# A two-layer 5-tap scan network on one core: the identity made first, weights loaded further on, the first group's lower rows stored further on, and the second quarter of a right scan loaded from ScalarE's queue

## The chip, the cores and the metric

One NeuronCore of a Trainium2 chip. The metric is the device time in microseconds (us) of the whole kernel, lower is better. Everything is 32-bit floating point.

## The reference

The input `x` is 32 images of 48 channels, 64 rows and 128 columns. Two layers of the same form follow each other; the core of one is

```python
def step(w, b):
    def f(carry, inp):
        nxt = inp + conv1d(carry, w, b)     # 5 taps along the line, 48 x 48 channels
        return (nxt, nxt)
    return f
D = scan(step(down_w, down_b), rows 1..63 of gn(x))          # from row 0 down
U = scan(step(down_w, down_b), back over D, rows 62..0)      # and up again
R = scan(step(right_w, right_b), columns 1..127 of U)        # from column 0 right
L = scan(step(left_w, left_b), back over R)                  # and left again
x = x + L
```

where `gn` is a group normalization over 16 groups of channels for each image. A scan is serial: a row (or column) needs the one before it, convolved along its length. In one layer there are 126 row steps and 254 column steps.

## The kernel before

**Groups and phases.** The images are cut into four groups of 8. A row scan handles one group (`rows`, layer, group): the three output tiles of a step are 128 x 128 matmuls, nine products for a step (`PRODUCTS`), and three VectorE instructions (L660) add bias and input and write the row back into SBUF, from where the next step reads it. A column scan handles a pair of groups (`cols`, layer, pair). `PHASES` lists the order: rows of groups 0 and 1, columns of pair 0, rows of group 2 in layer 0, rows of group 0 in layer 1 and so on, twelve phases in all. A row phase has 126 steps, a column phase 254; the text counts steps through the whole program (phase 1 begins after step 126, phase 2 after 252, phase 3 after 506, phase 6 after 884, phase 7 after 1138). In the profile a step's PSUM tile is named after layer, group or pair and direction: `step_00d`, `step_00u` are layer 0, group 0, down and up; `step_00r`, `step_00l` are layer 0, pair 0, right and left.

**Order of the work.** Around the scan everything else (loads, stores, statistics, normalization) is put on an agenda: `at(t, fn, ...)` says before which step a piece of work is written into the program. `in_order` keeps the program's order on each engine, so a piece never overtakes an earlier one on the same engine or DMA queue; the time t of a piece is only its place in that order. An engine or queue that has work behind its t runs late, and one that is ahead of its t may run a piece as soon as its inputs are there. Nearly all DMAs are issued from SyncE (SP, all at L193), a few from ScalarE (ACT). The program uses eight completion semaphores for these DMAs in turn, whichever of the two issues them, so that at most about eight are under way.

**Storage.** Three slots in SBUF hold 32 rows each in a row phase, or a quarter (32 columns of both groups) each in a column phase. A row phase takes its rows from DRAM (`xin` or `mid`) with `move_rows`, 20 DMAs for 16 rows, normalizes them on ScalarE with `scale_rows` (L536), and stores the scanned rows to `upa` or `upb` with `move_rows(..., True)`, 10 DMAs for 8 rows. A column phase loads quarters from `upa`/`upb` with `load_unit`, six units of three or four DMAs for a quarter. Where a column phase directly follows the rows of its second group (`follows(k)`: phases 2 and 6), the part of quarter 0 that belongs to that group is loaded from ScalarE's queue row by row as the rows come to be stored; the last two rows' part is written at t0, the phase's beginning. Quarter 1 is then loaded from SyncE's queue: units of the first group at t0 + 0.5, of the second at t0 + 1.5. It is needed from step 32 of the phase on, quarter 2 (written at t0 + 8 and on) from step 64.

**The beginning.** `first_group` (below) brings in group 0 by itself: its 32 loads of 16 rows (`take`), the identity in DRAM (`ident`), from which the pieces of a permutation are loaded into the space of the right and left weights (`wright<-ident`, `wleft<-ident`), the down weights (`taps`, then `downs`), constants, statistics (L340), a permutation by matmul (L987) and by copies (L493) into `xin`. The other groups are brought in by `plan_input`, in pieces at given times: a load (`take_in`), copies on GpSimd (L493) followed by stores to `xin`, and `lag` steps after a piece's time the statistics, for group 1 half of the images on VectorE (L340) and half on ScalarE (L350, L358).

**Weights.** `load_weights` issues five DMAs into a table in DRAM (`taps<-in_w`), a GpSimd memset of the weight tile (L232), and ten DMAs from the table into the tile, which wait for the five.

Of the kernel before, what the change touches and what calls it, by code (L numbers as in the profile page):

```python
# [33 lines left out]
C = 48  # L34
# [8 lines left out]
E8 = 8  # L43
# [4 lines left out]
DOWN, RIGHT, LEFT = range(3)  # L48
# [43 lines left out]
def kernel(  # L92
# [8 lines left out]
    nc = tc.nc  # L101
    B, _, H, W = x.shape
    NK = W // E8
    NH = H // E8
# [7 lines left out]
    HALF = H // 2  # L112
# [20 lines left out]
    def const(shape, name):  # L133
        return cpool.tile(shape, F32, tag=name, name=name)
# [12 lines left out]
    last = const([FULL, NG * N], "last")  # L147
# [44 lines left out]
    def dma(dst, src, queue=None):  # L192
        (queue or nc.sync).dma_start(dst, src)  # L193
# [314 lines left out]
    def row(k, h):  # L508
        return row_views(k)[h // HALF][:, :, h % HALF]
# [42 lines left out]
    def quarter(k, j):  # L552
        return slot[slots(k)[j % 3]].rearrange("p (o s n) -> p s o n", s=2, o=NG)
# [176 lines left out]
    def at(t, fn, *args):  # L730
        agenda.append((t, len(agenda), fn, args))
# [33 lines left out]
    def plan_rows(k, t0, prev):  # L765
        if k == 1:
            ahead, scaled = (-34, -18, 2, 18), (-14, -2, 17, 33)
        elif prev == "cols":
            ahead, scaled = (-28, -12, 4, 20), (-13, 3, 19, 35)
        else:  # L770
            ahead, scaled = (-54, -43, 0, 11), (-22, -8, 16, 30)
        if k:
            for i in range(4):
                at(t0 + ahead[i], move_rows, k, i * LOAD, (i + 1) * LOAD, False)
                at(t0 + scaled[i], scale_rows, k, i * LOAD, (i + 1) * LOAD)

        cuts = list(range(0, H + 1, E8))
        following = PHASES[k + 1][0] == "cols"
        if following and follows(k + 1):
            cuts = [0, E8 // 4] + cuts[1:]  # L780
        for h0, h1 in zip(cuts, cuts[1:]):
            t = t0 + 2 * (H - 1) - h0
            if k == 0:
                t += 24 if h0 >= HALF else 40
            elif not following:
                t = t0 + 92 + 5 * (H - h1) / E8 + (34 if h1 <= HALF else 0)
            at(t, move_rows, k, h0, h1, True)
        at(
            t0 + H - 1,
            nc.gpsimd.tensor_copy,  # L790
            last.rearrange("p (o n) -> p o n", o=NG),
            row(k, H - 1),
        )

    def follows(k):

        _, layer, pair = PHASES[k]
        return PHASES[k - 1] == ("rows", layer, 2 * pair + 1)

    def plan_cols(k, t0, prev):  # L800
        _, layer, pair = PHASES[k]
        n = 2 * NG
        after = prev == "cols"
        for i in range(n):
            if follows(k) and UNITS[i][1] == 1:
                other = nc.scalar
                at(t0 - 31 + i, load_unit, k, 0, i, 4, NH, 0, E8, other)
                at(t0 - 13 + i, load_unit, k, 0, i, 2, 4, 0, E8, other)
                at(t0 - 6 + i / n, load_unit, k, 0, i, 1, 2, 0, E8, other)
                at(t0 - 1.5, load_unit, k, 0, i, 0, 1, E8 // 4, E8, other)  # L810
                at(t0, load_unit, k, 0, i, 0, 1, 0, E8 // 4, other)
                at(t0 + 1.5, load_unit, k, 1, i)
            else:
                early = 30 if after else 46 if k == 2 else 70
                at(t0 - early + 2 * i, load_unit, k, 0, i)
                at(t0 + (3 if after else 0.5 if follows(k) else -24 + 2 * i), load_unit, k, 1, i)
            at(t0 + (38 if after else 8) + 2 * i, load_unit, k, 2, i)
            at(t0 + 33 + 2 * i, spill_unit, k, i, False)
            at(t0 + 50 + 2 * i, load_unit, k, 3, i)
        final = k == len(PHASES) - 1  # L820
        left = t0 + W - 1
        end = left + W - 1
        for i in range(n):
            at(left + 64 + 2 * i, spill_unit, k, i, True)
        units = []
        for n_done, j in enumerate((3, 2, 1, 0)):
            every = 4.5
            if j == 0 and PHASES[k + 1 if not final else k][0] == "rows":
                every = 7
            units += [(left + 34 + 32 * n_done + every * i, j, i) for i in range(n)]  # L830
        stats = None
        if layer == 0:
            stats = ResultStatsV(f"r{2 * pair}"), ResultStatsA(f"r{2 * pair + 1}")
        tiles = [stage[:, i] for i in range(4)]
        if layer:
            tiles.append(spare_tile)
        n = len(tiles)
        direct = [u for u in units if not (final and u[1] == 0)]

        for u, (t, j, i) in enumerate(direct):  # L840
            nat = tiles[u % n]
            o, half = UNITS[i]
            if u < n:
                at(left + 16, load_residual, k, j, i, nat)
            if layer == 0:
                if u >= n:
                    at(direct[u - n][0] + 3, load_residual, k, j, i, nat)
                at(t, add_residual, k, j, i, nat)
                at(t + 4, keep_result, k, j, i)
                unit = quarter(k, j)[:, half, o]  # L850
                if half == 0:
                    for b in range(GB):
                        at(t + 5 + b, stats[0].take, j, o, unit, b)
                else:
                    at(t + 1, stats[1].take, j, o, unit)
            else:

                at(t, add_residual, k, j, i, nat)
                at(t + 2.5, permute_unit, k, j, i, nat, (nc.gpsimd, nc.scalar, nc.scalar))
                if final or j not in HELD:  # L860
                    at(t + 4.5, store_result, k, j, i, nat)
                else:
                    at(t + 4.5, hold_result, j, i, nat)

                if u >= 2 and u - 2 + n < len(direct):
                    at(t + 4.6, load_residual, k, *direct[u - 2 + n][1:], tiles[(u - 2) % n])
        if layer == 0:
            t = units[-1][0] + 14
            g = 2 * pair
            spread(t, scaling(f"r{g}", 1, g, stats[0], r_masks), 1)  # L870
            spread(t + 20, scaling(f"r{g + 1}", 1, g + 1, stats[1], r_masks), 1)
        if layer:

            at(left + 10, nc.scalar.copy, junk[:, 0:1], quarter(k, 3)[:, 0, 0, RUN - 1 : RUN])
        if layer and not final:
            todo = [(j, half, e) for j in HELD for half in range(2) for e in range(E8)]
            for n, what in enumerate(todo):
                at(end + 63 + 1.9 * n, let_result, *what)
        if final:
            at(left + 97, last_loads, k)  # L880
            at(end + 4, last_results, k)
# [19 lines left out]
    starts = [0]  # L901
# [5 lines left out]
    def wide_nat(i0, n):  # L907
        return arena[0:P, i0 : i0 + GB * n * W].rearrange("p (b m) -> p b m", b=GB)

    tiles = [stage[0:P, i] for i in range(4)]  # L910
    nats1 = [wide_nat(2 * SLOT + i * UNIT * 4, 8) for i in range(2)]
    plan_input(1, [starts[0] + 38 + 13 * j for j in range(4)], 11, 5, nats1, tiles[2:4])
    nats = [wide_nat(3 * SLOT, 4)]
    times = [starts[2] + 16 + 13.5 * j for j in range(8)]
    plan_input(2, times, 6, 6, nats, tiles[2:4])
# [3 lines left out]
    def more_weights(key, layer, way):  # L919
        load_weights(key, layer, way)  # L920

    at(starts[1] + 20, more_weights, "right", 0, RIGHT)
    at(starts[1] + 24, more_weights, "left", 0, LEFT)
    at(starts[3] + 10, more_weights, "down1", 1, DOWN)
    at(starts[7] + 50, more_weights, "right", 1, RIGHT)
    at(starts[7] + 54, more_weights, "left", 1, LEFT)

# [1 line left out]
    def first_group():  # L929
# [10 lines left out]
        spare = {k: wt[k].rearrange("p i n -> p (i n)") for k in ("down1", "right", "left")}  # L940
        to_row = [spare["right"][0:C, i * FULL : (i + 1) * FULL] for i in range(9)]
        to_row += [spare["left"][0:C, 0:FULL]]
        one = last[0:C, 0 : C + 1]
        ident = dram.tile([C, C + 1], F32, tag="ident", name="ident")
        square = ident.rearrange("c n -> (c n)")[0 : C * C].rearrange("(c n) -> c n", n=C)

        def make_ident():
            nc.vector.memset(one, 0.0)
            nc.vector.memset(spare["right"], 0.0)
            nc.vector.memset(spare["left"], 0.0)  # L950
            dma(ident, one)
            nc.vector.memset(one[:, 0:1], 1.0)
            dma(ident[:, 0:1], one[:, 0:1])
            for m, (e, c0, c1, o, p0) in zip(to_row, PIECES):
                hold(m[c0:c1, p0 : p0 + c1 - c0], square[c0:c1, c0:c1])

        rows = HALF // 2
        parts = [wide_nat(SLOT + i * 2 * HALF * N * 2, rows) for i in range(2)]
        for b in range(2 * GB):
            i, b = divmod(b, GB)  # L960
            (nc.vector if b % 2 else nc.gpsimd).memset(parts[i][32:64, b], 0.0)

# [165 lines left out]
```

## Time and profile before

| | us |
|---|---|
| median of 3 runs (lowest to highest) | 4429.61 (4427.96 to 4435.4) |
| the profiled execution | 4442.85 |
| its span, first to last instruction | 4441.1 |
| TensorE busy in the span | 4160.7 (94%) |
| VectorE, ScalarE, GpSimd busy | 2184.7, 1311.7, 828.6 |
| DMA of SyncE's queue (q1), of ScalarE's (q10): MB, share of 16 DMA engines' time | 599.07, 70.8%; 75.51, 6.9% |
| first step of the scan starts at, last one ends at | 108.60, 4336.4 |
| phases 0 and 1: from the first step to the last | 108.6 to 680.1 |
| phase 2 | 706.0 to 1221.7 |
| phase 3 | 1221.6 to 1493.0 |
| phases 4 and 5 | 1493.0 to 2001.3 |
| phase 6 | 2024.8 to 2538.0 |

The span is one profiled execution's. A matmul row of the timeline stands for many instructions without a break, and the bracket at its end tells how long the engine had been idle before, and what ended it. A row of SyncE or ScalarE with a q tells when DMAs were issued, not when they landed; landings are in the list of DMA issues. A phase that runs without a stop takes 2.01 us a step: 126.63 us for 63 steps in phases 3 to 5.

### The profile page before, as it was taken

The numbers are of one execution on the slowest core, as the hardware profiler recorded it, in microseconds if no ns is written. First come the engines' busy times: TensorE is split into PE (matmuls) and PEld (weight loads), VectorE is DVE, ScalarE is ACT, GpSimd is POOL, SyncE is SP. The second block draws the span as 40 slices with busy tenths as digits, with TensorE's granted clock in tenths as the row PEclk, the third lists the DMA queues.
The fourth block names the chain that finished last, engine by engine and source line by source line (L and its number), as shares of the span: only waits on it lengthen the run. The fifth ranks groups of instructions, "written<-read, shape, count | busy, mean of one in ns | idle before, by whom it ended". The sixth has DMA issues, their size and how long they took to land.

```text
span 4441.1 us, 89969 instructions
## 1 busy us (share of the span) xinstructions
PE 4160.7 (94%) x36632; PEld 4130.6 (93%) x36632; DVE 2184.7 (49%) x6594; ACT 1311.7 (30%) x2570; POOL 828.6 (19%) x775
## 2 busy tenths in 40 slices
PE   3889997999999999997999999999999999999990
PEld 1889997999999999997999999999999999999990
DVE  5355443446655444443446665444444444444442
ACT  1752301434785554200005774503000011110112
POOL 3442000323323020000004310000000034410443
PEclk9999998999999999998999999999999999999995
DMA  8988879865997989678406989839187059999899
GB/s 170 179 166 153 132 136 185 217 129 168 238 197 135 157 154 161 99 123 200 87 1 214 224 171 142 133 56 170 32 139 176 1 96 228 249 242 159 142 217 150
DMA packets 2111229, 680.33 MB, mean 153 GB/s; under 512 B 2000992, under 2 KB 2053984, under 8 KB 2070880
## 3 DMA queue, kind: packets, MB, share of 16 engines
q1 hardware_dynamic: 2095168, 599.07, 70.8%
q10 hardware_dynamic: 15648, 75.51, 6.9%
q8 instruction: 288, 4.72, 0.5%
q14 instruction: 125, 1.02, 0.1%
HBM read 397.57 MB, written 295.98 MB: 156 GB/s over the span
## 4 chain that ended last, share of the span: by engine, by line
PE 84%; DMA 6%; SPq 4%; ACT 2%; DVE 1%; issue 1%; POOL 1%; ACTq 0%; POOLq 0%; DVEq 0%
PE step_00r L651 6%; PE step_01r L651 6%; PE step_10r L651 6%; PE step_00l L651 6%; PE step_10l L651 6%; PE step_01l L651 6%; SPq L193 4%; PE step_11r L651 4%; PE step_11l L651 4%; PE step_10u L651 3%; PE step_11u L651 3%; PE step_13d L651 3%; PE step_12u L651 3%; PE step_12d L651 3%; PE step_03d L651 3%; PE step_10d L651 3%
## 5 line engine op out<-in xcount | busy, mean ns | idle before, releaser
L536 ACT ACTIVATE arena<-arena,offset,scale 128x256 f32<-128x256 f32 (+2 forms) x864 | 601.4, 790 | 441.1 <-DMA arena<-xin 146.0
L589 POOL TENSOR_TENSOR arena<-arena 128x2048 f32<-128x2048 f32 x83 | 376.4, 4549 | 1743.6 <-PE step_01l L651 508.5
L493 POOL COPY arena<-arena 112x256 f32<-112x256 f32 x458 | 270.5, 647 | 760.5 <-DMA arena<-in_x 495.9
L427 ACT ACTIVATE junk<-arena 128x256 f32<-128x256 f32 x192 | 129.5, 675 | 692.2 <-DMA arena<-xin 552.1
L651 PE MATMUL step_00r<-arena,wright 128*128 128x128 f32 x2286 | 258.7, 277 | 25.9 <-DMA arena<-upa 25.9
L651 PEld LDWEIGHTS step_00r<-arena,wright 128*128 128x128 f32 x2286 | 258.3, 194 | 26.3 <-issue 26.1
L651 PE MATMUL step_01r<-arena,wright 128*128 128x128 f32 x2286 | 258.0, 276 | 23.5 <-DMA arena<-upa 23.5
L651 PEld LDWEIGHTS step_01r<-arena,wright 128*128 128x128 f32 x2286 | 257.7, 193 | 23.9 <-issue 23.7
L651 PE MATMUL step_11r<-arena,wright 128*128 128x128 f32 x2286 | 259.1, 277 | 4.3 <-DVE arena L660 4.3
L651 PEld LDWEIGHTS step_11r<-arena,wright 128*128 128x128 f32 x2286 | 258.4, 194 | 4.8 <-DVE arena L660 4.5
L651 PE MATMUL step_00l<-arena,wleft 128*128 128x128 f32 x2286 | 256.3, 275 | 0.0
L651 PE MATMUL step_10r<-arena,wright 128*128 128x128 f32 x2286 | 256.0, 275 | 0.0
L651 PEld LDWEIGHTS step_10r<-arena,wright 128*128 128x128 f32 x2286 | 255.7, 192 | 0.3
L651 PEld LDWEIGHTS step_00l<-arena,wleft 128*128 128x128 f32 x2286 | 255.7, 192 | 0.0
L651 PE MATMUL step_11l<-arena,wleft 128*128 128x128 f32 x2286 | 255.5, 275 | 0.0
L651 PE MATMUL step_10l<-arena,wleft 128*128 128x128 f32 x2286 | 255.5, 275 | 0.0
L651 PE MATMUL step_01l<-arena,wleft 128*128 128x128 f32 x2286 | 255.4, 275 | 0.0
L651 PEld LDWEIGHTS step_11l<-arena,wleft 128*128 128x128 f32 x2286 | 255.4, 192 | 0.0
L651 PEld LDWEIGHTS step_10l<-arena,wleft 128*128 128x128 f32 x2286 | 255.4, 192 | 0.0
L651 PEld LDWEIGHTS step_01l<-arena,wleft 128*128 128x128 f32 x2286 | 255.3, 192 | 0.0
L614 ACT COPY arena<-arena 128x256 f32<-128x256 f32 x190 | 109.7, 655 | 477.2 <-POOL arena L589 215.4
L358 ACT ACTIVATE junk<-arena 112x512 f32<-112x512 f32 x160 | 100.9, 631 | 491.0 <-DMA arena<-in_x 486.6
(177 smaller groups left out, 7037.0 us busy)
## 6 DMA issues: line engine op xcount, KB each, us to landing
xin<-arena SPq DMA_DIRECT2D x96, 384.0 KB, 5.4
arena<-xin SPq DMA_DIRECT2D x96, 384.0 KB, 8.6
mid<-arena SPq DMA_DIRECT2D x96, 384.0 KB, 7.8
arena<-mid SPq DMA_DIRECT2D x192, 192.0 KB, 4.4
upb<-arena SPq DMA_DIRECT2D x192, 192.0 KB, 3.9
arena<-upb SPq DMA_DIRECT2D x96, 384.0 KB, 11.2
arena<-xin SPq DMA_DIRECT2D x186, 192.0 KB, 4.3
upa<-arena SPq DMA_DIRECT2D x180, 192.0 KB, 3.9
```

What stands on the lines that cost most here:

```text
L193: (queue or nc.sync).dma_start(dst, src)
L358: nc.scalar.activation(junk[0:P], piece, AF.Identity, accum_out=self.sum[:, at[0], at[1]],)
L427: nc.scalar.activation(junk[:, 0:n], view[:, b], AF.Identity, accum_out=self.sum[:, i, j : j + 1])
L493: copy(dst[:, r, q], src[:, r0 + r, q])
L536: nc.scalar.activation(args[0], args[0], AF.Identity, bias=args[2], scale=args[1])
L589: eng.tensor_tensor(unit, unit, nat, ALU.add)
L614: copy(by_w(perm)[:, a], src[:, a])
L651: nc.tensor.matmul(part(whole(ps[o]), -s), weights[:, i, FULL * (o - NG * s - i + 1) : FULL * (o - NG * s - i + 2)], part(src(i), s), star ...
```

## The change

- In `first_group` the two memsets for the identity (zeros and ones, now in two places of the tile `last`) come before all other memsets, and the memsets of the right and left weights' space after the first two of the sixteen memsets of the padding. The DMAs that write the identity to DRAM stand where they stood, after the first six loads.
- `move_rows` of the first group's rows below 32 to DRAM: 28 steps further on (its 40 DMAs at steps 170 to 194 instead of 142 to 166).
- The right and left weights of layer 0: 30 steps further on (steps 176 and 180 instead of 146 and 150). The down weights of layer 1: at step 556 instead of 516.
- Group 1's statistics: two steps further on (`lag` 7 instead of 5). By the formulas in `plan_input` the loads of its last two pieces are written one step further on, and its scaling two.
- In phases 2 and 6 all of quarter 1 (20 DMAs, 6 MB) is loaded from ScalarE's queue at t0 + 1.5.

```diff
-                t += 24 if h0 >= HALF else 40
+                t += 24 if h0 >= HALF else 68
...
                 at(t0, load_unit, k, 0, i, 0, 1, 0, E8 // 4, other)
-                at(t0 + 1.5, load_unit, k, 1, i)
             else:
                 early = 30 if after else 46 if k == 2 else 70
                 at(t0 - early + 2 * i, load_unit, k, 0, i)
-                at(t0 + (3 if after else 0.5 if follows(k) else -24 + 2 * i), load_unit, k, 1, i)
+            if follows(k):
+                at(t0 + 1.5, load_unit, k, 1, i, 0, NH, 0, E8, nc.scalar)
+            else:
+                at(t0 + (3 if after else -24 + 2 * i), load_unit, k, 1, i)
...
-    plan_input(1, [starts[0] + 38 + 13 * j for j in range(4)], 11, 5, nats1, tiles[2:4])
+    plan_input(1, [starts[0] + 38 + 13 * j for j in range(4)], 11, 7, nats1, tiles[2:4])
...
-    at(starts[1] + 20, more_weights, "right", 0, RIGHT)
-    at(starts[1] + 24, more_weights, "left", 0, LEFT)
-    at(starts[3] + 10, more_weights, "down1", 1, DOWN)
+    at(starts[1] + 50, more_weights, "right", 0, RIGHT)
+    at(starts[1] + 54, more_weights, "left", 0, LEFT)
+    at(starts[3] + 50, more_weights, "down1", 1, DOWN)
...
-        one = last[0:C, 0 : C + 1]
+        zero, one = last[0:C, 0 : C + 1], last[0:C, C + 1 : C + 2]
...
         def make_ident():
-            nc.vector.memset(one, 0.0)
-            nc.vector.memset(spare["right"], 0.0)
-            nc.vector.memset(spare["left"], 0.0)
-            dma(ident, one)
-            nc.vector.memset(one[:, 0:1], 1.0)
-            dma(ident[:, 0:1], one[:, 0:1])
+            dma(ident, zero)
+            dma(ident[:, 0:1], one)
...
         parts = [wide_nat(SLOT + i * 2 * HALF * N * 2, rows) for i in range(2)]
+        nc.vector.memset(zero, 0.0)
+        nc.vector.memset(one, 1.0)
         for b in range(2 * GB):
+            if b == 2:
+                nc.vector.memset(spare["right"], 0.0)
+                nc.vector.memset(spare["left"], 0.0)
             i, b = divmod(b, GB)
             (nc.vector if b % 2 else nc.gpsimd).memset(parts[i][32:64, b], 0.0)
```

## The prediction

> **What bounds the kernel now.** I read the page's first lines, then TensorE's waits, then the places of those waits in the timeline and the list of DMA issues.
>
> ```profile
> span 4441.1 us, 89969 instructions
> ...
> PE 4160.7 (94%) x36632; PEld 4130.6 (93%) x36632; DVE 2184.7 (49%) x6594; ACT 1311.7 (30%) x2570; POOL 828.6 (19%) x775
> ```
>
> The scan is a chain of matmul and VectorE add, 2.01 us a step, and the change touches no step. Only the places where TensorE stands still can move. Its waits (total, times, longest):
>
> ```profile
> PE step_00r L651 <- DMA arena<-upa: 25.9, 1, 25.9
> PE step_01r L651 <- DMA arena<-upa: 23.5, 1, 23.5
> PE step_00d L651 <- DVE arena L660: 21.1, 3, 10.7
> ...
> PE step_00u L651 <- DVE arena L660: 9.5, 1, 9.5
> PE step_02d L651 <- DVE arena L660: 9.3, 1, 9.3
> PE step_01d L651 <- issue: 6.5, 1, 6.5
> PE step_01d L651 <- DVE arena L660: 5.8, 1, 5.8
> ```
>
> The first two are the openings of column phases 2 and 6. In phase 2 TensorE starts at 706.04; the chain of waits ends there with a load issued at 695.37 that took 10.58. The DMA issues of 694.98 to 695.9 (KB, median us to landing), and ScalarE's of 691 to 692.4:
>
> ```profile
> arena<-upa SPq DMA_DIRECT2D x2, 384.0 KB, 10.8
> ...
> arena<-upa ACTq DMA_DIRECT2D x2, 48.0 KB, 9.5
> ```
> ```profile
> arena<-upa ACTq DMA_DIRECT2D x2, 48.0 KB, 2.0
> ```
>
> The same small load lands in 2.0 us, and in 9.5 once SyncE has begun its 384 KB loads of quarter 1 (from 693.37). These 48 KB, not quarter 1, are what the first step needs. Phase 6 is alike: its two 48 KB loads took a median 8.3.
>
> The 9.3 us belong to phase 3, step 48. SyncE's queue ahead of it:
>
> ```profile
> 1268.72 5.94 SPq L193 DMA_DIRECT2D taps<-in_w  x5
> 1276.70 4.50 SPq L193 DMA_DIRECT2D downs<-taps  x10
> ```
>
> Weights take 1268.72 to 1281.25, then come three residual loads, three stores, and from 1287.02 the rows 48 to 63, landed at 1312.2, whose scaling on ScalarE (22 of 24 instructions, 16.33 us) ends at 1328.5. TensorE had been ready at 1318.2.
>
> The head (SyncE) and phase 1 (SyncE):
>
> ```profile
> 2.56 2.73 SPq L193 DMA_DIRECT2D arena<-in_x  x6
> 18.16 2.75 SPq L193 DMA_DIRECT2D ident<-last  x2
> 21.97 1.23 SPq L193 DMA_DIRECT2D wright<-ident  x3
> ```
> ```profile
> 364.31 23.49 SPq L193 DMA_DIRECT2D arena<-xin  x20
> 387.85 20.99 SPq L193 DMA_DIRECT2D upa<-arena  x20
> 408.88 20.85 SPq L193 DMA_DIRECT2D arena<-xin  x20
> 429.78 19.43 SPq L193 DMA_DIRECT2D upa<-arena  x20
> 449.30 20.80 SPq L193 DMA_DIRECT2D arena<-xin  x20
> ```
>
> In phase 1 SyncE issues without a break; rows 16 to 31 come in the third line, rows 32 to 47 in the fifth, and the two stalls of step_01d (at 441.4 and 482.6) end one ScalarE scaling after those lines end.
>
> **What the Trainium skill says.** "DMA: Bandwidth & Descriptors", section "Issuing engines are not separate DMA queues": transfers issued by SyncE and ScalarE run on the same 16 engines and interleave. The trace agrees: 2.0 us alone, 9.5 beside SyncE's loads. So another queue alone buys nothing; what counts is who stands ahead. Same page, "Queues, rings and completion order": each engine alternates between the queues' rings, a whole packet at a time, and takes its own ring in order. A load issued behind the small ones on ScalarE's ring therefore doesn't delay them much; in the head, where one queue works, landings do follow the issues. "TensorE: Matmul & The Clock Gate", Part 1: after an idle window of about 3.4 us the array runs at half rate until it has been busy as long. Agrees: after the 9.28 us of phase 3 seven steps took 17.11 us where 7 x 2.01 = 14.1.
>
> **The change, part by part.**
>
> *Identity.* Before, SyncE waits from 5.3 (six loads issued) to 18.16 for VectorE's memset behind eight padding memsets, then for two small DMAs in turn (1.35 and 1.31 us to landing), until 21.97. After, the memset costs 0.1 us at the start, and the first small DMA is issued at 5.3; but it stands behind six loads of which the last landed at 17.28. By the spacing of small landings behind big ones (0.4 to 0.5) it lands at 17.7. The second still waits for it: 17.7 + 1.35 = 19.1. Gain 21.97 - 19.1 = **2.9**. All that follows in the head is one SyncE chain (its next loads landed back to back to 45, and the first step waits on statistics of the last load), so the 2.9 reach the first step, and the stalls of steps 16 and 32, whose rows hang on the same SyncE chain, shift with it. Bounds: 0 (something else fills 19 to 22) and 4.3 (the second doesn't wait).
>
> *lag.* At step 43 VectorE waited 5.3 us for a load (landed 224.9) with the scan's adds behind it; likewise at step 82 (9.5, landed 316.4). Two steps later is 2 x 2.01 = 4.0 us less stall each. But this gain isn't kept: loads, copies and stores of group 1 run ahead of these statistics on SyncE and GpSimd alone and don't wait for TensorE; the lines from 364.31 on start when GpSimd's last copy ends (363.4). TensorE arrives earlier at steps 142 and 158 and waits that much longer. Value **0**; bounds +7 (the two restarts as well) and -3 (one more cold restart, at phase 1's start). The one-step shifts of the two loads pass nothing on SyncE (50 before a store at 50.25, 63 before 63.25); scaling ends at step 110, before its use at 112.
>
> *Lower rows and right/left weights.* 40 stores and 2 x 15 weight DMAs on SyncE pass only the load of rows 48 to 63 (the 20 DMAs written at step 144), which come some 10 us sooner; their step 174 had no stall, so nothing. The sum of SyncE's work up to step 196 is the same, and there it waited 16.0 us (551.1 to 567.0) for the scan: that hides it. Beyond 16 us of delay the stores of phase 1's last rows would slip one for one. The GpSimd memsets (1.06 us each) stay ahead of the copy to `last` at 553.98. Value **0**, bounds -3, +3.
>
> *Down weights.* Out of phase 3's chain: 1281.25 - 1268.72 = 12.5 us. Rows 48 to 63 then land at about 1299.7; ScalarE is free of statistics at 1297.2; scaling ends near 1300 + 16.4 = 1316.4, before TensorE's 1318.2. So up to the whole stall goes: 9.28 idle and 3.0 of slow steps = 12.3. Phase 7 is the same pattern without weights: its scaling of these rows ended 98.9 us after its start (phase 3: 106.9) and it still lost 1.35 + 0.25 idle + 2.1 slow = 3.7, which would leave 12.3 - 3.7 = 8.6. I take the middle, **10.5**; what is late next is this same scaling. At step 556 the weights' 12.5 us fall into a hole of SyncE (1356 to 1373, waiting for GpSimd's copies); without it group 3's input slips by as much. The memset lies between GpSimd copies there.
>
> *Quarter 1.* SyncE's large loads no longer run beside the last small ones. These land after some 2.3 us (2.0 for 48 KB, 2.5 for 32 KB beside stores): phase 2 10.58 - 2.3 = **8.3**; phase 6 9.4 (2014.99 to 2024.38) - 2.3 = **7.1**. ScalarE now issues 20 DMAs from 695.8, each waiting for one of eight completion semaphores. Behind them on ScalarE stands only group 2's statistics, whose load landed at 745.9; in phase 6 nothing for long. Quarter 1 landed at 735.8, needed at 697.8 + 31 x 2.01 = 760: cover 24 us. SyncE's quarter 2 would be next, but needs semaphores that quarter 1 holds. Bounds for each: 0 (still interleaved) and 8.6.
>
> Sum: 2.9 + 0 + 0 + 10.5 + 8.3 + 7.1 = **28.8** us. The profiled execution took 4442.85 (span 4441.1 and 1.75 around it), so it would take 4414.0; the median stands 13.2 below that execution, so 4429.6 - 28.8 = 4400.8.
>
> **Rivals.** (a) Phase 1 gains too: its two stalls (6.5 and 5.8 idle) are not SyncE's chain and vanish: 4400.8 - 12.3 = 4388. For: SyncE's order does change there. Against: only behind rows 32 to 47. (b) The openings keep their contention (same DMA engines, quarter 1 right behind): 4400.8 + 15.4 = 4416. Against: order within a ring. (c) Phase 3's wait is also replaced by another, with (b): only the head, 4429.6 - 2.9 = 4427. (d) Slower than before: SyncE, free of quarter 1, starts quarter 2 at once; both share the engines, so quarter 1 takes 2 x 42.4 us (693.4 to 735.8) and ends at 695.8 + 84.8 = 781, against 760: 21 us of stall at step 32 in phases 2 and 6, 42 - 28.8 = 13 slower, 4443. It decides from 28.8 / 2 = 14.4 us of lateness. For: nothing in SyncE's own order holds quarter 2 back. Against: the shared semaphores; SyncE's loads of that time do wait on ScalarE's.
>
> **Numbers.** 0.2% is 8.9 us, about what a measurement can tell from no change. Likeliest 0.62 (4392 to 4411), (a) 0.10, (b) 0.14, (c) 0.08, (d) 0.06. Faster 0.86, same 0.08, slower 0.06. The range 4386 to 4417 holds the first three, most of the tails aside.
>
> **What would show it.** Right: wright<-ident at about 19, first step near 105.7; TensorE idle about 17.5 before step_00r and 16 before step_01r, small ScalarE loads landing in 2 to 3 us; no gap in step_02d; step_01d still stalling, more than before. Wrong: a stall at step 32 of step_00r, SyncE's wait before step 196 gone, or gaps in step_10d because group 3's input is late.

## The result, and the profile after

The changed kernel takes 4416.33 us (median of 7 runs, 4405.48 to 4417.81), the kernel before 4429.61 in the 7 runs taken beside it (4426.7 to 4440.98). The ratio is 0.9959, 95% interval 0.9945 to 0.9973: about 18 us or 0.4% faster by the ratio, 12 to 24 by its interval; the medians differ by 13.3. The profiled executions are 4442.85 (before) and 4416.53 (after). The one of before lies 13 above its median, so what the pair of profiles differs by (26 us) is more than the change is worth: 3.7 us of it lie in phase 7, which no edit touches (262.1 us in the profile before, 258.3 to 259.3 in the thirteen others). Where it matters I use the traces of the other kernels below, most of which run the code of before in the place concerned.

The page of the changed kernel, its first line and its engines (busy us, share, instructions), and ScalarE's DMA queue (packets, MB, share of the 16 engines):

```profile
span 4414.7 us, 89966 instructions
...
PE 4154.9 (94%) x36632; PEld 4125.1 (93%) x36632; DVE 2183.1 (49%) x6594; ACT 1311.1 (30%) x2570; POOL 829.0 (19%) x775
...
q10 hardware_dynamic: 17824, 88.10, 8.4%
```

The work is the same. ScalarE's queue carries 12.6 MB more than before (75.51 MB), the quarter 1 of two phases. TensorE's waits after the change (us in total, times, longest):

```profile
PE step_00r L651 <- DMA arena<-upa: 21.1, 1, 21.1
PE step_01r L651 <- DMA arena<-upa: 20.8, 1, 20.8
PE step_00d L651 <- DVE arena L660: 16.4, 3, 10.1
PE step_00u L651 <- DVE arena L660: 11.7, 1, 11.7
PE step_01d L651 <- issue: 9.5, 1, 9.5
...
PE step_01d L651 <- DVE arena L660: 4.8, 1, 4.8
PE step_02u L651 <- DVE arena L660: 2.6, 1, 2.6
```

Three things are to be seen. The openings of phases 2 and 6 are shorter (25.9 and 23.5 before) but not the 17.5 and 16 that I had forecast. The gap in step_02d is gone, and there is a new, small one in step_02u. In phases 0 and 1 the waits have only changed places: step_00d 4.7 less, step_00u 2.2 and step_01d 2.0 more.

Why the openings stop half-way is in the DMA issues of 687.2 to 690, ahead of phase 2's first step (KB each, median us from issue to landing):

```profile
arena<-upa SPq DMA_DIRECT2D x2, 384.0 KB, 5.0
arena<-upa ACTq DMA_DIRECT2D x1, 384.0 KB, 7.2
arena<-upa SPq DMA_DIRECT2D x1, 256.0 KB, 6.1
arena<-upa ACTq DMA_DIRECT2D x2, 48.0 KB, 6.1
```

The last line is the pair of small loads that the first step of phase 2 waits for. Alone such a pair took 2.0 us, in the profile before 9.5, and here 6.1, because SyncE has again begun large loads ahead of it. They are no longer quarter 1 but the first three of quarter 2. The timeline of SyncE in the changed kernel (start, duration of the stretch, count):

```profile
683.93 3.26 SPq L193 DMA_DIRECT2D upa<-arena  x4
687.29 1.73 SPq L193 DMA_DIRECT2D arena<-upa  x3
691.83 5.72 SPq L193 DMA_DIRECT2D arena<-in_x  x2
```

The small loads were issued at 689.09 and 689.44, two microseconds after SyncE went on to quarter 2. They landed at 695.15 and 695.50, just after the last of SyncE's three loads (694.67).

### The profile page after: what moved, and what is told of

The parts are those of the page before. It is cut to its first block, busy times and chain, and to the rows that moved or that the text cites. A ratio compares the mean times of both kernels' runs of the same rounds, so it can differ in the third digit from the quotient of the medians.

```text
span 4414.7 us, 89966 instructions
## 1 busy us (share of the span) xinstructions
PE 4154.9 (94%) x36632; PEld 4125.1 (93%) x36632; DVE 2183.1 (49%) x6594; ACT 1311.1 (30%) x2570; POOL 829.0 (19%) x775
## 4 chain that ended last, share of the span: by engine, by line
PE 85%; DMA 6%; ACT 4%; SPq 3%; issue 1%; POOL 1%; DVE 0%; ACTq 0%; POOLq 0%; DVEq 0%
PE step_01r L651 6%; PE step_00r L651 6%; PE step_10r L651 6%; PE step_00l L651 6%; PE step_10l L651 6%; PE step_01l L651 6%; PE step_11l L651 5%; PE step_11r L651 4%; PE step_11d L651 3%; PE step_10u L651 3%; PE step_11u L651 3%; PE step_12d L651 3%; PE step_13u L651 3%; PE step_12u L651 3%; PE step_13d L651 3%; PE step_03d L651 3%
## 5 line engine op out<-in xcount | busy, mean ns | idle before, releaser
L651 PE MATMUL step_00r<-arena,wright 128*128 128x128 f32 x2286 | 257.7, 276 | 21.1 <-DMA arena<-upa 21.1
L651 PEld LDWEIGHTS step_00r<-arena,wright 128*128 128x128 f32 x2286 | 257.5, 193 | 21.3 <-issue 21.2
L651 PEld LDWEIGHTS step_11r<-arena,wright 128*128 128x128 f32 x2286 | 258.3, 193 | 5.5 <-DVE arena L660 5.3
```

The costliest lines, as they stand in the source:

```text
L651: nc.tensor.matmul(part(whole(ps[o]), -s), weights[:, i, FULL * (o - NG * s - i + 1) : FULL * (o - NG * s - i + 2)], part(src(i), s), star ...
```

## The experiments

Each kernel below was timed beside the kernel before, in three batches: the first four kernels, the next four, and the last four. The median of the kernel before was 4426.3, 4429.9 and 4424.4 us in them, so kernels of different batches are compared by their ratios. A difference in us is the ratio's, taken of 4427 us, with its 95% interval.

**Only quarter 1 on ScalarE's queue.**

```diff
-                at(t0 + 1.5, load_unit, k, 1, i)
...
-                at(t0 + (3 if after else 0.5 if follows(k) else -24 + 2 * i), load_unit, k, 1, i)
+            if follows(k):
+                at(t0 + 1.5, load_unit, k, 1, i, 0, NH, 0, E8, nc.scalar)
+            else:
+                at(t0 + (3 if after else -24 + 2 * i), load_unit, k, 1, i)
```

> Only quarter 1 of phases 2 and 6 goes to ScalarE's queue; the rest as before. Theory 1 (half of the contention stays, because SyncE, freed of quarter 1, issues quarter 2 ahead of the two 48 KB loads): idle before step_00r and step_01r about 21 us each, the 48 KB loads landing in about 6 us, time 7 to 8 us below before. Theory 2 (the step as predicted, SyncE held back by semaphores): 17.5 and 16 us idle, 15.4 us below before. Theory 3 (the shorter openings seen after the whole change come from its other parts): no difference.

Measured: 4415.35 us, ratio 0.9978 (0.9969 to 0.9986), 9.7 us faster (6 to 14). TensorE's waits at the two openings, and the small loads (queue, KB, us to landing):

```profile
PE step_01r L651 <- DMA arena<-upa: 21.9, 1, 21.9
...
PE step_00r L651 <- DMA arena<-upa: 20.9, 1, 20.9
```
```profile
arena<-upa SPq DMA_DIRECT2D x2, 384.0 KB, 5.0
arena<-upa SPq DMA_DIRECT2D x1, 256.0 KB, 6.2
arena<-upa ACTq DMA_DIRECT2D x2, 48.0 KB, 5.9
```

The shorter openings come from this part alone, and they stop at the same place as in the whole change. Theory 1 holds, theories 2 and 3 fall.

**Large loads held back, queue unchanged.** Quarter 1 stays on SyncE's queue as before. Ahead of it stands one DMA that copies two elements, one of each of the two small loads, to a spare place in DRAM. It must wait until both have landed, and since SyncE issues in order, so must everything behind it. Nothing reads its result.

```diff
+    gate_to = dram.tile([2, 1], F32, tag="gate", name="gate")
+    def gate(k):
+        dma(gate_to, quarter(k, 0)[C - 1 : C + 1, 1, 0, 0:1])
...
+        if follows(k):
+            at(t0 + 0.1, gate, k)
+        for i in range(n):
```

> As before, quarter 1 on SyncE's queue, but ahead of it on that queue one tiny DMA that reads one element of each of the two 48 KB loads, so that SyncE starts nothing until they have landed. Theory 1 (any large load that SyncE has under way is what makes the small ones late, whichever quarter it is): the 48 KB loads land in 2 to 2.5 us, idle about 17.5 and 16 us, time about 15 us below before; quarter 1 starts some 4 us later than before and is still in time for step 32. Rival (the queue is what counts, large loads must leave SyncE): idle stays above 20 us, at most 8 us below before. Rival (quarter 1 comes too late): a stall at step 32 of step_00r and step_01r, no gain.

Measured: 4412.05 us, ratio 0.9966 (0.9952 to 0.9979), 15 us faster (9 to 21). TensorE's waits, SyncE's timeline, and the small loads:

```profile
PE step_00r L651 <- DMA arena<-upa: 17.0, 1, 17.0
PE step_01r L651 <- DMA gate<-arena: 15.9, 1, 15.9
```
```profile
690.33 0.29 SPq L193 DMA_DIRECT2D gate<-arena  x1
690.72 10.72 SPq L193 DMA_DIRECT2D arena<-upa  x13
```
```profile
arena<-upa ACTq DMA_DIRECT2D x2, 48.0 KB, 1.7
```

The second small load landed at 690.26, the tiny DMA was issued at 690.33, quarter 1 from 690.72 on. With no large load under way the small ones take 1.7 us, and the idle times are the 17.5 and 16 of the prediction within half a microsecond. (In the second line the wait is put down to the tiny DMA because it is the last thing the profile saw; it waits for the same small loads.) So what counts is whether large loads are under way when the small ones are issued; moving them to another queue isn't needed. Quarter 1 starts 0.5 us after the landing, some 4 us later against the small loads than in the profile before, and brought no stall at step 32.

**The same tiny DMA in the changed kernel.** The edit is that of the kernel above, made in the changed one.

> The changed kernel with the same tiny DMA on SyncE's queue ahead of quarter 2, so that SyncE starts quarter 2 and group 2's input only when the two 48 KB loads have landed; quarter 1 stays on ScalarE's queue right behind them. Theory 1: the 48 KB loads land in 2 to 2.5 us, idle about 17 us in both openings, 8 us below the changed kernel, 20 to 22 below before. Rival (loads behind the small ones on their own ring slow them too): landing 4 us or more, idle about 20 us, no more than 2 us below the changed kernel.

Measured: 4401.91 us, ratio to before 0.9942 (0.9929 to 0.9955), 26 us faster than before. Its waits and the DMA issues of 690 to 693.65:

```profile
PE step_00r L651 <- DMA arena<-upa: 16.9, 1, 16.9
...
PE step_01r L651 <- DMA gate<-arena: 15.8, 1, 15.8
```
```profile
arena<-upa ACTq DMA_DIRECT2D x3, 384.0 KB, 6.0
arena<-upa ACTq DMA_DIRECT2D x1, 256.0 KB
arena<-upa ACTq DMA_DIRECT2D x2, 48.0 KB, 1.8
```

Here loads of quarter 1 (the first two lines) stand right behind the small ones on the same queue; three of the four were issued, from 692.0 on, before the second small one landed at 693.24, and it still took 1.8 us. This fits what the Trainium skill says in "DMA: Bandwidth & Descriptors", section "Queues, rings and completion order": an engine takes a ring in order and alternates between rings. The rival falls: large loads behind on the small ones' own ring cost nothing here. Large loads ahead on the other ring do cost, and more than an alternation would make one expect: in all nine traces with such loads the later of the two small ones, for which the step waits, lands only after the first three of them. Why they wait for these no run shows, and none has large loads behind the small ones on the other ring alone.

This kernel also shows the price of quarter 1 on ScalarE's queue: at step 32 of phase 2 VectorE waits 0.67 us for a load of quarter 1, and the step takes 2.40 us instead of 2.01.

**Only the down weights of layer 1 at step 556.**

```diff
-    at(starts[3] + 10, more_weights, "down1", 1, DOWN)
+    at(starts[3] + 50, more_weights, "down1", 1, DOWN)
```

> Only the down weights of layer 1 are loaded at step 556 instead of 516. Theory 1: the gap of 9.3 us in step_02d goes with its restart (12 us), and 4 us of that come back as a stall in step_02u near step 591, where VectorE waits for constants that stand behind group 3's late statistics on ScalarE: 8 us below before. Rival (the stall after the whole change has another cause, such as the shifted phases): 12 us below before and no gap in step_02u. Rival (the rows are late for another reason): a gap in step_02d stays.

Measured: 4420.19 us, ratio 0.9988 (0.998 to 0.9995), 5 us faster (2 to 9). No gap in step_02d; in step_02u:

```profile
PE step_02u L651 <- DVE arena L660: 0.8, 1, 0.8
```

Theory 1 holds for the gap that goes and for the existence of one that comes back; its size varies (0.8 here, 2.6 in the changed kernel, 0.5 and 1.3 in two others with the weights at 556, none in two more). How it arises shows best in the changed kernel, SyncE's timeline there, and then the instructions of ScalarE, VectorE and TensorE:

```profile
1334.00 3.15 SPq L193 DMA_DIRECT2D taps<-in_w  x5
1347.40 4.51 SPq L193 DMA_DIRECT2D downs<-taps  x10
1352.01 6.82 SPq L193 DMA_DIRECT2D xin<-arena  x4
1359.43 2.18 SPq L193 DMA_DIRECT2D arena<-in_x  x2
```
```profile
1387.57 0.21 ACT L303 ACTIVATE std_r<-var_r 128x24 f32<-128x24 f32 x1
1387.81 0.30 DVE L307 RECIPROCAL std_r<-std_r 128x24 f32<-128x24 f32 x1 [3.15 <-ACT std_r L303]
1388.87 3.37 PE L651 MATMUL step_02u<-arena,downs 128*128 128x128 f32 x16 [2.58 <-DVE arena L660]
```

The weights stand ahead of group 3's stores and load. The load issued from 1359.43 on lands at 1374.52, about 3 us later against the scan's steps than in the profile before. ScalarE's statistics of it then run until 1387.5, and the square root for the next group's constants (L303) stands behind them. VectorE waits 3.15 us for that, with the scan's adds queued behind its own wait.

Phase 3 as a whole, from the end of step 506 to the end of step 632, took 271.3 us in the profile before, but 266.9 to 268.2 in the seven other traces with the weights at 516. With them at 556 it took 262.9 in the changed kernel, 258.5 to 259.9 in four others, 261.9 in one. So the part is worth some 7 to 8 us, and the profile before happened to take about 4 us more there than the seven others.

**Only the identity first.**

```diff
         def make_ident():
-            nc.vector.memset(one, 0.0)
...
-            dma(ident, one)
-            nc.vector.memset(one[:, 0:1], 1.0)
-            dma(ident[:, 0:1], one[:, 0:1])
+            dma(ident, zero)
+            dma(ident[:, 0:1], one)
...
+        nc.vector.memset(zero, 0.0)
+        nc.vector.memset(one, 1.0)
         for b in range(2 * GB):
...
```

> Only the identity is made first. The step as predicted: the whole chain of the head comes 2.9 us sooner and so does the end, 2.9 us below before. Theory after the runs so far (in runs with the head of before the first step came at 105.1 to 105.8 us, with the new head at 104.2 and 105.0, because loads of 16 rows that start sooner are spaced wider): the first pieces of the permutation land 2 us sooner, the first step about 0.8 us, and the time is within 1.5 us of before. A first step that comes 4 us sooner than 105.5 would show that the head gave what the two first profiles differ by.

Measured: 4422.75 us, ratio 0.9984 (0.9975 to 0.9993), 7 us faster (3 to 11). SyncE's timeline at its start:

```profile
5.34 13.90 SPq L193 DMA_DIRECT2D ident<-last  x2
20.32 1.23 SPq L193 DMA_DIRECT2D wright<-ident  x3
21.65 0.83 SPq L193 DMA_DIRECT2D arena<-in_x  x2
```

The mechanism is as predicted: the first small DMA is issued at 5.3, behind the six loads, and wright<-ident comes 1.6 us sooner than in the profile before (21.97); in the five traces with the new head it comes 1.6 to 2.9 sooner. What is left of that at the first step is hard to see. It ends at 108.4 to 111.7 (mean 109.5) with the new head, and at 108.4 to 115.2 (mean 111.1) in nine traces with the old one; with the same instructions, the last of the head's loads landed anywhere from 87.8 to 94.5. The means differ by 1.6 us, with a spread that makes this no more than a hint. The time says more (3 to 11), and no place in the trace that the edit touches accounts for the rest; the kernel with the tiny DMA, the down weights and the identity, below, looks at it again.

**Only the statistics two steps later.**

```diff
-    plan_input(1, [starts[0] + 38 + 13 * j for j in range(4)], 11, 5, nats1, tiles[2:4])
+    plan_input(1, [starts[0] + 38 + 13 * j for j in range(4)], 11, 7, nats1, tiles[2:4])
```

> Only group 1's statistics two steps further on (and with them its last two loads by one, its scaling by two). Theory 1 (SyncE's chain of group 1's loads and stores sets when phase 1 ends): the gap of 5 to 6 us in step_00d near step 44 shrinks to about 2, the first gap of step_01d grows by the same, phase 1 ends as before (672 to 676) and the time is within 2 us of before. Rival (the stalls of phase 0 are worth their length): 4 to 7 us below before.

Measured: 4428.32 us, ratio 0.9999 (0.9991 to 1.0007). Its waits in phases 0 and 1:

```profile
PE step_00d L651 <- DVE arena L660: 14.9, 3, 9.7
PE step_00u L651 <- DVE arena L660: 12.9, 1, 12.9
PE step_01d L651 <- issue: 7.8, 1, 7.8
```

Before they were 21.1, 9.5 and 6.5: most of what the first loses the others get. Phase 0 is 4 to 5 us shorter (291.4 us from the end of the first step to the end of step 126, against 294.8 to 297.3 in nine traces with the old lag) and phase 1 as much longer (274.6 against 267.0 to 270.9). That the gain isn't kept is as predicted. But the stall near step 84 (step_00u), which the prediction had shrink by 4 us as well, grew: to 11.7 to 13.3 us in the five traces with the new lag, from 8.4 to 10.6.

**Only the lower rows and the right and left weights later.**

```diff
-                t += 24 if h0 >= HALF else 40
+                t += 24 if h0 >= HALF else 68
...
-    at(starts[1] + 20, more_weights, "right", 0, RIGHT)
-    at(starts[1] + 24, more_weights, "left", 0, LEFT)
+    at(starts[1] + 50, more_weights, "right", 0, RIGHT)
+    at(starts[1] + 54, more_weights, "left", 0, LEFT)
```

> Only the first group's lower rows are stored 28 steps later and the right and left weights loaded 30 steps later. As predicted: no difference, since SyncE does the same work up to step 196 and waits there. Rival (rows 48 to 63 come sooner, so the second gap of step_01d shrinks): 3 to 5 us below before. Rival (the loads of phase 1's rows run without the stores between them, the later stores and weights push the last stores of phase 1): phase 1 or the opening of phase 2 ends 2 to 4 us later than in before.

Measured: 4428.49 us, ratio 0.9999 (0.999 to 1.0007): no difference, as predicted.

**The tiny DMA and the down weights, nothing else.** The two edits shown above, in the kernel before.

> As before, with the tiny DMA on SyncE's queue ahead of quarter 1 and the down weights at step 556, and nothing else of the change. If these two alone hold the gain: 20 us below before (14 and 6, each measured alone), 4404 to 4406, within 4 us of the changed kernel with the tiny DMA (24 below before). If lag, rows and identity were worth something together, it stays 3 us or more above that one.

Measured: 4403.02 us, ratio 0.9940 (0.9927 to 0.9952), 27 us faster than before (21 to 32). Measured alone the two gave 15 and 5, which sums to a little less than that interval; by the traces it is 17.9 (openings) and 7 to 8 (phase 3). These two hold the whole gain of the changed kernel with the tiny DMA (26). With or without the other parts it is one time, within the intervals, and about 8 us below the changed kernel by the ratios; the interval of that one (0.9945 to 0.9973) just overlaps.

The same with the identity first:

> The tiny DMA ahead of quarter 1, the down weights at step 556, and the identity made first. If the identity is worth what it gave alone: 3 to 7 us below the same kernel without it (4403.0), so 4396 to 4400. If the first pieces of the permutation come 2 us sooner but the loads behind them are spaced wider: 1 us, 4402.

Measured: 4399.27 us, ratio 0.9942 (0.993 to 0.9955), against 0.9940 without it. The median falls where the first case had it, but in this batch the kernel before is 5.5 us lower too (4424.4 against 4429.9), and by the ratios nothing is to be seen of the identity. I count it at 1 to 2 us, an estimate from the first step above, and leave open why alone it measured more.

**Another order of SyncE's chain in phase 1.** If the order of loads and stores is what makes step_01d stall, another order of the same DMAs must remove both gaps.

```diff
-                t += 24 if h0 >= HALF else 40
+                t += 60 if h0 >= 48 else 24 if h0 >= HALF else 40
```

> As before, but the stores of the first group's rows 48 to 63 come after the loads of group 1's rows 16 to 31 and 32 to 47 on SyncE's queue instead of ahead of them (their space isn't needed before rows 48 to 63 are loaded). No work is added or taken away. Theory 1 (SyncE's order of loads and stores sets the two gaps of step_01d): rows 16 to 31 land 20 us sooner, rows 32 to 47 too, both gaps go with their restarts, phase 1 ends about 12 us sooner, unless rows 48 to 63 are late next; time 9 to 13 us below before. Rival (the gaps have to do with ScalarE's scaling or with the amount of SyncE's work up to step 196): within 3 us of before.

Measured: 4427.58 us, ratio 1.0003 (0.9995 to 1.0011): no gain. SyncE's timeline and TensorE's one wait in step_01d:

```profile
364.52 43.78 SPq L193 DMA_DIRECT2D arena<-xin  x40
408.35 20.80 SPq L193 DMA_DIRECT2D upa<-arena  x20
429.25 19.82 SPq L193 DMA_DIRECT2D arena<-xin  x20
449.11 30.94 SPq L193 DMA_DIRECT2D upa<-arena  x30
480.10 21.89 SPq L193 DMA_DIRECT2D arena<-xin  x20
```
```profile
PE step_01d L651 <- DVE arena L660: 14.1, 1, 14.1
```

Both gaps are gone, as theory 1 said: rows 16 to 31 and 32 to 47 come 20 us sooner. But a single gap of 14.1 has taken their place, at step 174, where rows 48 to 63 are now late: their load starts at 480.1, behind the 20 postponed stores and 10 stores of lower rows. I had allowed for that with "unless rows 48 to 63 are late next" and not worked it out; the number that I expected was wrong. From the first load of this chain to the end of phase 1 it is 312 to 316 us in all fourteen traces, with either lag, either place of the lower rows and either order of the stores. So it looks as if SyncE's chain as a whole sets that end; this is argued from the sameness of that stretch, and no run made the chain shorter. Moving the lower rows alone leaves the two gaps of rows 16 to 47 (4.5 and 5.8 us), the new order alone leaves rows 48 to 63 late; both together might give what neither does. That was not tried.

The same order with the later statistics (the lag's edit above):

> The kernel of the run before this one, and group 1's statistics two steps further on. Theory 1 (what the later statistics gain in phase 0 is lost only because SyncE's loads of phase 1 don't come sooner): now the gain stays, 3 to 5 us below the run before this one. Rival (the gain is lost within phase 0, at the gap near step 85): no difference to it.

Measured: 4428.85 us, ratio 1.0011 (1.0002 to 1.0019), 5 us slower than before. The order alone was at 1.0003 (0.9995 to 1.0011), so theory 1 falls: there is no gain of 3 to 5 us over it, and the two intervals overlap. Phases 0 and 1 together took 563.7 us against 565.5 for the order alone, but the execution profiled was 4 us below the median of its kernel. Whether the later statistics cost something here stays open; they gain nothing.

And all that had helped or might, in one kernel (five of the edits above):

> Everything that helped: the tiny DMA ahead of quarter 1, the down weights at step 556, the identity first, group 1's statistics two steps later, and the stores of the first group's rows 48 to 63 behind the loads of group 1's rows 16 to 47. If the parts add: 27 (gate and down weights), 9 to 13 (order), 3 to 5 (statistics) and 1 to 7 (identity) below before, 4380 to 4390. If phase 1 has another bound next: 4395 or more.

Measured: 4406.57 us, ratio 0.995 (0.9936 to 0.9963), 22 us faster than before. Phase 1 had another bound next, as the second case said: the gap of step 174 again, 15.9 us here. In phase 3 gaps of 1.1 us (step_02d) and 1.3 (step_02u) were left. It is no better than the tiny DMA and the down weights alone.

## Why the prediction was right, and where it was not

The forecast was 4400.8, the measurement 4416.3: faster as forecast and inside the range, but 15 us off, outside the likeliest stretch (4392 to 4411) and 0.7 us from the end of the range. The gain was 18 us by the ratio where 28.8 were forecast. That it still lies in the range owes something to luck: the range was drawn to take in rival (b). By its steps:

- **Quarter 1, 8.3 + 7.1 us.** The mechanism was right: the small loads take 1.7 us without large ones beside them, and the idle times then are 17.0 and 15.9. The step that failed is "SyncE's quarter 2 would be next, but needs semaphores that quarter 1 holds". In the trace the loads of the two queues alternate in taking the eight semaphores: quarter 2's first three loads take those of three transfers that had landed by 685.7, 688.2 and 688.5, and were issued at 687.29, 688.24 and 688.60, while the first three of quarter 1 took the semaphores in between. So next to nothing held SyncE. I had named this in rival (d) ("nothing in SyncE's own order holds quarter 2 back") and believed the other side. From the end of the last step to the end of the first of the new phase, the seven traces with quarter 1 on SyncE's queue took 30.8 and 28.2 us on average, the two with it on ScalarE's 25.0 and 25.5, the five with the tiny DMA 21.2 and 19.9. The part gave 5.8 + 2.7 = 8.5, not 15.4; the tiny DMA gives 17.9.
- **Rival (b)** forecast the measured time, 4416, but for a reason that half holds: quarter 1 right behind on the same queue costs nothing, and quarter 2 on the other queue costs about half. **Rival (d)** did not decide, but only just. In phase 2 quarter 1's last load landed at 759.7, and step 32, which needs it, ended at 762.6; in the profile before these were 735.8 and 773.7. Its reason was right, that the two quarters share the DMA engines: from its first issue to its last landing quarter 1 took 69.7 us, before 42.4. The cover that the prediction put at 24 us came down to under 3; with the tiny DMA added, 0.4 us of stall do show there. That no stall came in the changed kernel is luck.
- **Down weights, 10.5 us.** Right in mechanism, too large by about 3: the seven other traces with the weights at 516 took about 4 us less in phase 3 than the one I read. The evidence that had me take off 2 us, the 3.7 us that phase 7 lost without weights, was that profile's own: the thirteen others took 2.8 to 3.8 us less there. And the hole of SyncE at step 556 wasn't quite free, with up to 4.4 us (2.6 idle and two slow steps) coming back at step 591. I had said "without it group 3's input slips by as much", and it slipped by 3. (After the 9.3 us gap in the profile before, the granted clock was 0.50 for 5.5 us, longer than the 3.4 us that the prediction names, and then 1.00.)
- **Identity, 2.9 us.** Its DMAs came 1.6 to 2.9 us sooner (wright<-ident at 20.1 in the changed kernel, forecast about 19); about 1.6 arrives at the first step, by the means. The 4.4 us between the two profiles there (108.6 and 104.2) are mostly the scatter of the head. That the identity alone measured 3 to 11 stays open.
- **Lag, lower rows, right and left weights: 0.** Both measured at 0.4 us (within 4 either way). For the lag the gain is given back in phase 1, as said, but part of it already at the stall near step 84, which the prediction had expected to shrink.

Together the sizes from the traces are 8.5 + 7.5 + 1.6 = 18 us, which is what the ratio says (18, 12 to 24). Of the 15.5 us between forecast and median 6.9 are the openings, 3 the weights, 1.3 the identity; the other 4 to 5 are what the two medians differ by less (13.3) than the ratio says. Rivals (a) and (c) are out: phase 1 gained nothing, and phase 3's wait did go.

## What to carry to other kernels

Before large loads are moved off a queue to make way for a small urgent one, ask what that queue will do next: it runs on to its next large load unless something holds it. A two-element DMA that reads what the urgent load brings is such a hold. It let the queue go on half a microsecond after the landing, put the large loads back by some 4 us, for which there was cover here, and gave more than the move to the other queue did (17.9 us against 8.5 by the traces; by the times 15 against 10, with intervals that overlap). The move used up nearly all the cover of the loads that were moved, the hold did not. In phases 0 and 1, where one serial chain of transfers seems to set the end, shifting its pieces or the work in front of it moved the stalls and did not shorten them; look for what is late next on the same chain before counting the gain.

## What I had not expected of the hardware

The head's loads are the same instructions in nine traces with the old head, and the last landed between 87.8 and 94.5 us; the first step moved with it. A single profile of this kernel can't tell a change of 3 us there. The other end scatters as much: from the end of the last step to the end of the kernel, which no edit touches, it is 96.2 to 104.3 us in the fourteen traces. And a 48 KB load that takes 1.6 to 2.0 us with no large load ahead of it (five traces) takes 5.9 to 7.4 behind three loads of 256 to 384 KB that were begun on the other queue in the two microseconds before. In the seven traces where that queue went on with quarter 1, three to five loads ahead and more right behind, it takes 7.1 to 12.0.
